# Bilinear features from 33 correlations of the value map instead of a second mixing convolution

## The chip, the cores and the metric

The kernel runs on one core of one Trainium2 chip, in float32 throughout. The metric is the device time of one execution in microseconds (us). Before the change three executions took 12944.30, 12963.82 and 12975.63 us, median 12963.82 us.

## The reference, cut to what matters

An input of 16 images of 56 x 56 tokens with 128 channels goes through four residual layers: windowed attention (stage 0), a triangle multiplication (stage 1), a Fourier attention block (stage 2) and a bilinear block (stage 3). The change touches stage 3, and how stage 1 gets four of its weights. Stage 3 for one image:

```python
xp = jax.nn.silu(x @ W1) @ W2                     # 128 q, 16 k, 16 v channels
q, k, v = l2norm(q per 16), l2norm(k), l2norm(v)  # 8 heads of q; k and v: 16 channels each
K_H1 = conv2d(k, H1_w, groups=16) + P1            # 3x7 window, 256 channels: (16, 16) per token
kernel = einsum('xnk,xkd->xnd', q, K_H1)          # (8, 16) per token
feature = conv2d(v, H2_w)                         # (v=16, d=16) per token
V_G = conv2d(v, G_w) + I                          # (v=16, w=16) per token
feature = einsum('xvw,xvd->xwd', V_G, feature)
out = einsum('xnd,xvd->xvn', kernel, feature)     # (16, 8) per token
```

Both convolutions of v are shared by all 16 value channels: every channel v is convolved with the same 16 filters H2 and the same 16 filters G. The feature is thus feature[w,d] = sum over v of (I[v,w] + sum_s G[w,s] v_v(x+s)) * (sum_t H2[d,t] v_v(x+t)). The part without I needs only sums over the channels, sum_v v_v(x+s) v_v(x+t): these are values at position x+s of a correlation map with the lag t-s. A 3 x 7 window has 5 x 13 lags, 33 of them up to sign.

## The kernel before, in words

Two images are worked on at a time, one in each of two **lanes** (lane 0: images 0, 2, ...; lane 1: images 1, 3, ...). A lane has its own large SBUF buffer (`arena`, 128 x 17152 float32, one buffer, given anew to every stage of every image), its own small buffers (`w2`, five of 128 x 512), its own PSUM banks (two of `psb`, one double bank `psd`) and its own DRAM tiles. The program is written image by image; a scheduler with a timeline model then sets the order of the instructions on each engine, and so interleaves the two lanes. Each engine, and each engine's DMA queue, takes its instructions in that order. DMAs that SyncE (SP) and ScalarE (ACT) ask for draw in turn on eight semaphores, DMAHW0 to DMAHW7, and one that gets a semaphore waits until the DMA that had it before, eight issues back, has landed. GpSimd's (POOL's) table DMAs have eight of their own.

Stage 3 cuts an image into seven chunks of 448 tokens (eight image rows). The steps by name, with line numbers of the kernel before:

- `project(q)` (1345 to 1401): normalizes, W1, SiLU, W2. The q channels go through `kept` (1338): a copy to SBUF by ACT and one DMA that writes them eight times to DRAM (`dy`, 1792 KB). The k and v channels are squared, summed, raised to the power -0.5 on POOL (417), scaled (1380), turned by TensorE (1388), and written by three ACT DMAs (1397), one per window row, into a zero-edged image in DRAM, `padded`.
- `spread(i, q)` (1403): four SP DMAs bring 84 shifted rows each of the k (i=0) or v (i=1) image into `im`, the moving operand of the convolutions.
- `conv(w, i, slot)` (1411): TensorE applies `l3wk` (k with H1 and P1), `l3wf` (v with H2) or `l3wg` (v with G and I) to 896 results per token, and ACT empties them into `zs` (1427). `l3wk` and `l3wg` run as groups of four 32-column matmuls side by side (`e.together`, lines 369 and 372); `l3wf` runs with all 128 columns (1420).
- `contract(y, z)` (1430): the per-token product and sum. Four SP DMAs (1439, 448 KB each) bring `dy` back as `rep`, replicated over partitions; four VectorE (DVE) multiplies of 128 x 1792 (1442) multiply it by `z`; sixteen 32-column matmuls with the constant `red` (369, 372) add up.
- `last(q, y, z)` (1457): the third contraction, transposes, scaling by the norm, residual and store.

Per chunk there are three contractions, chained: queries with zk, that with zf (the kernel with the feature's H2 factor), that with zg. Two of the results go through `kept` besides the queries, so each chunk has three `dy` writes and twelve `rep` reads. The loop of 1484 to 1500 spaces these over five rounds: chunk q is projected two rounds ahead, and contracted in rounds q, q+2 and q+4.

Stage 1 reads its weights `w1a`, `w1b`, `pout`, `gout` from the one weight tile `wgt` that is loaded at the start and stays in SBUF.

Of the kernel before, what the change touches and what calls it, by code (L numbers as in the profile page):

```python
# [36 lines left out]
F32 = mybir.dt.float32  # L37
# [55 lines left out]

def _constants():
# [31 lines left out]
    c["heads"] = np.kron(np.eye(8), np.ones((16, 1)))  # L126

# [78 lines left out]
def _weights(i):  # L206
# [15 lines left out]
    for n, (a, b) in zip("ab", cut):  # L222
        w["w1" + n] = np.concatenate([pw[:, a], pw[:, b], gw[:, a], gw[:, b]], 1)
    w["pout"] = g["L1_conv_p_out_w"].T
    w["gout"] = g["L1_conv_g_out_w"].T
# [48 lines left out]
    w["l3w2a"] = g["L3_conv_W2"][:128]  # L274
    w["l3w2b"] = np.pad(g["L3_conv_W2"][128:], ((0, 96), (0, 0)))
# [5 lines left out]
    wk3, wg3 = (np.zeros((P, 4, 2, 4, 8), np.float32) for _ in range(2))  # L281
    wf3 = np.zeros((P, 4, 16, 8), np.float32)
    for u in range(16):
        rows = slice(u % 4 * 21, u % 4 * 21 + 21)
        wk3[rows, u // 4, :, u % 4] = h1[u].reshape(2, 8, 21).transpose(2, 0, 1)
        wg3[rows, u // 4, :, u % 4] = gg.reshape(2, 8, 21).transpose(2, 0, 1)
        wf3[rows, u // 4, :, u % 8] = h2.reshape(16, 21).T
    wk3[84] = g["L3_conv_P1"][0].reshape(4, 4, 2, 8).transpose(0, 2, 1, 3)
    wg3[84] = g["L3_conv_I"][0].reshape(4, 4, 2, 8).transpose(0, 2, 1, 3)
    for n, v in (("l3wk", wk3), ("l3wf", wf3), ("l3wg", wg3)):  # L290
        w[n] = v.reshape(P, -1)
    return w, early, late
# [333 lines left out]
def _triangle(env):  # L626
# [5 lines left out]
    def layer_norm(chunk, dst, sqs, lw, lb):  # L632


        for q in range(NCH):
# [5 lines left out]
            nc.vector.tensor_copy(d, p[:, :CH])  # L641

# [22 lines left out]
    def run(b, xt):  # L665
# [3 lines left out]
        nc.gpsimd.memset(xh[:, NTOK:], 0.0)  # L669

# [6 lines left out]
        layer_norm(normed, xh, sqs, 0, 1)  # L677
# [5 lines left out]
        for part in range(2):  # L683
            for g in range(T // 8):
                p = e.psd()
                for i in range(8):
                    c0 = (8 * g + i) * T
                    for half, w in ((0, "w1a"), (64, "w1b")):
# [3 lines left out]
                            rhs=W(w).rearrange("p (k c) -> p k c", c=64)[:, :, HC * part : HC * part + HC],  # L692
# [34 lines left out]
        for q in range(NCH):  # L727
            s = slice(q * CH, (q + 1) * CH)
            pg, py = e.psb(), e.psb()
            mm(pg[:, :CH], lhsT=W("gout"), rhs=xh[:, s], start=True, stop=True)  # L730
            mm(py[:, :CH], lhsT=W("pout"), rhs=on[:, s], start=True, stop=True)
# [572 lines left out]
def _bilinear(env):  # L1304
# [6 lines left out]
    SPAN = 8 * PITCH  # L1311

# [3 lines left out]
    nc.gpsimd.memset(zeros[:, :part], 0.0)  # L1316
    for t in padded:
        for k in range(3):
            nc.sync.dma_start(out=t[:, k * part : (k + 1) * part], in_=zeros[:, :part])

# [4 lines left out]
    def run(b, xt):  # L1325
        nm, rs = e.group_norm(xt)
        ar = e.arena()
        kv_dram = padded[e.lane[0]]

        im = [ar[:, 4 * SPAN * k : 4 * SPAN * (k + 1)] for k in range(2)]  # L1330
        nc.gpsimd.memset(ar[64:P, 0 : 8 * SPAN], 1.0)
        zs = [ar[:, 3968 + k * 896 : 4864 + k * 896] for k in range(4)]
        reps = [ar[:, 7552 + k * 896 : 8448 + k * 896] for k in range(4)]
        prods = [ar[:, 11136 + k * 1792 : 12928 + k * 1792] for k in range(3)]
        norms = ar[:TT, 16512:16792]
        count = [0, 0, 0]

        def kept(p):
# [188 lines left out]
```

## Time and profile before

| | us |
|---|---|
| median of three runs | 12963.82 |
| the profiled execution | 12942.02 |
| its span, first to last instruction | 12940.2 |
| TensorE (PE) matmuls busy | 9941.9 (77%) |
| VectorE (DVE) busy | 9365.3 (72%) |
| ScalarE (ACT) busy | 3739.1 (29%) |
| GpSimd (POOL) busy | 2346.8 (18%) |
| DMA queue of SP | 823.91 MB, 19.1% of 16 DMA engines |
| DMA queue of ACT | 639.44 MB, 13.3% |
| DMA queue of POOL | 616.76 MB, 17.7% |
| DVE multiplies of the contractions (line 1442) | 2648.4, 1344 of 2019 ns |

The first column of the profile's page is busy time: an engine is busy while one of its instructions runs, and a PE that is busy need not be at its peak. The page also cuts the span into 40 slices and gives each engine's busy share in tenths; a view of windows gives the same in microseconds for stretches that one chooses. Every five slices (about 1612 us) one pair of images goes by: stages 0 and 1 (no DMA), stage 2 (the table DMAs of POOL), stage 3 (the DMAs of SP and ACT). Stage 3 of both lanes of a pair runs at the same time, from about 2650 to 3280 us for the second pair.

### The profile page before, as it was taken

How to read it: one execution, taken by the hardware profiler on the slowest of the kernel's cores; microseconds unless marked ns; L12 is line 12 of the kernel's file. 1: busy time of each engine (PE TensorE's matmuls, PEld its weight loads, DVE VectorE, ACT ScalarE, POOL GpSimd, SP SyncE). 2: the span in 40 equal slices, each digit the busy share in tenths (PEclk: the TensorE clock that was granted, in tenths of full speed). 3: DMA queues.
4: the chain of work that ended last, by engine and by line, in shares of the span. 5: the costliest groups of instructions: out<-in, count | busy, mean ns of one | idle time of the engine just before them, and what ended most of it. 6: DMA issues, size and time to landing. Idle time of an engine off the chain costs nothing. (4 is left out here: it accounts for less than half of the span.)

```text
span 12940.2 us, 198571 instructions
## 1 busy us (share of the span) xinstructions
PE 9941.9 (77%) x81312; PEld 5481.7 (42%) x81312; DVE 9365.3 (72%) x12257; ACT 3739.1 (29%) x6439; POOL 2346.8 (18%) x3131
## 2 busy tenths in 40 slices
PE   7787678876888767887788876878768887687876
PEld 4443254442544325443254432544325453254532
DVE  7775777757777577775877757777577775867757
ACT  4322142231422314223142231422314223142321
POOL 0133001330012300123101230012300123001230
PEclk9887888888988889888898888988889888898888
DMA  1255902659026590355903569035690356903469
GB/s 36 58 182 195 341 29 69 171 199 334 32 83 157 198 339 28 87 153 203 342 21 82 158 210 338 18 92 148 212 333 21 96 145 234 324 8 106 134 236 317
DMA packets 1090458, 2092.81 MB, mean 162 GB/s; under 512 B 97936, under 2 KB 973712, under 8 KB 1089296
## 3 DMA queue, kind: packets, MB, share of 16 engines
q1 hardware_dynamic: 560000, 823.91, 19.1%
q0 software_dynamic: 163840, 616.76, 17.7%
q10 hardware_dynamic: 365712, 639.44, 13.3%
q8 instruction: 644, 10.55, 0.3%
q14 instruction: 262, 2.15, 0.1%
HBM read 1412.69 MB, written 667.03 MB: 161 GB/s over the span
## 5 line engine op out<-in xcount | busy, mean ns | idle before, releaser
L1442 DVE TENSOR_TENSOR arena<-arena 128x1792 f32<-128x1792 f32 x1344 | 2648.4, 2019 | 652.5 <-PE psb L372 349.3
L1211 DVE TENSOR_TENSOR arena<-arena 112x1344 f32<-112x1344 f32 x1024 | 1563.3, 1552 | 322.4 <-DMA arena<-table 310.4
L372 PE MATMUL psb<-arena,cst 128*32 128x448 f32 x9792 | 1505.2, 649 | 0.0
L1209 POOL DMA_DIRECT2D arena<-table x2048 | 1050.7, 515 | 2206.3 <-DMA arena<-table 496.5
L369 PE MATMUL psb<-arena,cst 128*32 128x448 f32 x1408 | 792.3, 650 | 813.7 <-DVE arena L1442 760.4
L372 PE MATMUL psb<-arena 128*64 128x448 f32 (+2 forms) x4864 | 1248.5, 534 | 0.0
L369 PE MATMUL psb<-arena 112*64 112x448 f32 (+1 forms) x1280 | 689.0, 624 | 374.2 <-DVE arena L1104 201.9
L417 POOL TENSOR_TENSOR arena<-arena,power 112x32 f32<-112x32 f32 x224 | 828.6, 3718 | 119.8 <-DVE arena L1373 118.4
L372 PE MATMUL psd<-arena 112*64 112x224 f32 (+1 forms) x3072 | 725.6, 457 | 0.0
L372 PEld LDWEIGHTS psb<-arena 112*64 112x64 f32 (+1 forms) x4864 | 455.3, 155 | 526.8 <-issue 521.1
L1427 ACT COPY arena<-psd 128x896 f32<-128x896 f32 x336 | 304.1, 906 | 1236.1 <-DVE arena L1442 656.6
L369 PE MATMUL psd<-arena 112*64 112x448 f32 x1024 | 539.9, 612 | 133.3 <-DVE arena L1211 117.6
L369 PEld LDWEIGHTS psb<-arena,cst 128*32 128x32 f32 x1408 | 120.3, 118 | 1211.5 <-DVE arena L1442 966.4
L1104 DVE TENSOR_TENSOR arena<-w,coef 128x1792 f32<-128x1792 f32 x256 | 508.0, 2018 | 81.4 <-PE psb L372 71.0
L372 PEld LDWEIGHTS psb<-arena,cst 128*32 128x32 f32 x9792 | 360.6, 123 | 448.2 <-issue 427.4
L372 PE MATMUL psd<-arena,wgt 128*32 128x448 f32 x2688 | 502.8, 608 | 38.8 <-DMA arena<-padded 38.3
L689 PE MATMUL psd<-wgt,arena 128*64 128x128 f32 x7168 | 493.3, 283 | 49.3 <-DVE arena L701 38.9
L369 PE MATMUL psd<-arena,wgt 128*32 128x448 f32 x896 | 440.7, 611 | 79.9 <-DMA arena<-padded 42.2
L689 PEld LDWEIGHTS psd<-wgt,arena 128*64 128x64 f32 x7168 | 425.4, 139 | 179.5 <-issue 126.8
L918 PE MATMUL psb<-cst,arena 128*128 128x64 f32 (+1 forms) x2688 | 447.6, 340 | 54.3 <-ACT arena L928 25.6
L918 PEld LDWEIGHTS psb<-cst,arena 128*128 128x128 f32 x2688 | 439.0, 255 | 93.2 <-issue 50.6
L1341 ACT COPY w<-psb 128x448 f32<-128x448 f32 x336 | 178.7, 532 | 1006.5 <-PE psb L372 749.9
(305 smaller groups left out, 18845.8 us busy)
## 6 DMA issues: line engine op xcount, KB each, us to landing
arena<-table POOLq DMA_DIRECT2D x2048, 294.0 KB, 9.1
dy<-w ACTq DMA_DIRECT2D x336, 1792.0 KB
arena<-dy SPq DMA_DIRECT2D x1344, 448.0 KB
arena<-padded SPq DMA_DIRECT2D x896, 162.8 KB
w<-x SPq DMA_DIRECT2D x112, 224.0 KB
out<-w SPq DMA_DIRECT2D x112, 224.0 KB
padded<-w ACTq DMA_DIRECT2D x336, 62.0 KB
padded<-arena SPq DMA_DIRECT2D x6, 449.5 KB
```

The lines of the kernel that those rows point to most:

```text
L369: done = mm(**first)
L372: mm(**kw)
L417: ptt(dst, src, w, ALU.pow)
L689: mm(p[half : half + 64, i // 4, i % 4 * P : (i % 4 + 1) * P], lhsT=xh[:, c0 : c0 + 64], rhs=W(w).rearrange("p (k c) -> p k c", c=64)[:, : ...
L918: mm(p[:, 2 * i * nl : 2 * (i + 1) * nl], lhsT=src[:, t * P : (t + 1) * P], rhs=fc, start=True, stop=True)
L1104: tt(t4, bc(ys[c][:, l0 : l0 + 4, :], 1, 8), bc(coef[:, c, h0 : h0 + 8, l0 : l0 + 4], 3, T), ALU.mult,)
L1209: nc.gpsimd.dma_start(out=t[hh * T : (hh + 1) * T, :], in_=bc(tflat[q, two, hh], 0, T))
L1211: tt(t4, bc(x3[:, :, s], 1, 2), t4, ALU.mult)
L1341: nc.scalar.copy(t[:, :CH], p[:, :CH])
L1427: nc.scalar.copy(z, p[:, :, :CH])
L1442: tt(t4, bc(rep, 2, 2), bc(z, 1, 2), ALU.mult)
```

## The change

The contraction with zg goes. What it made is computed from the value map before any token's product is taken:

- W2's value columns are doubled: one copy keeps the plain v, one is multiplied by I at the start (`l3vt`, `l3i`), so that the H2 convolution works on v times I, and gives the I part of the feature by itself. `project` now carries 48 instead of 32 channels per token group, and writes the plain v by one more ACT DMA into a new DRAM tile, `values`, in eight copies, each shifted by one element against the one before.
- `correlate(q)`: one SP DMA brings the values of a chunk (128 partitions: 8 copies of 16 channels), six more bring 32 of the 33 lags, eight lags to a tile, straight from the shifted copies. ACT squares, DVE multiplies twice (128 x 992), and five matmuls with the constant `lag` add up the channels: 33 correlation rows of 496 elements, which ACT copies and writes to DRAM (`corr`).
- `gather(q)`: eight SP DMAs bring 126, 105 and 81 shifted rows of the correlations into three tiles `near`.
- `feature()`: the four `l3wf` matmuls as before, and six more with `quad` (products of G and H2, made by DVE at the start), added in the same PSUM banks; ACT empties them once.
- The loop does two contractions per chunk: queries with zk in round q, that with the feature in round q+3. `kept` is called twice per chunk instead of three times. `spread(0, q)` moves to the round's start, `gather` and `spread(1, .)` stand a round ahead of the `feature()` that reads them.
- Stage 1's four weights leave `wgt`. They are loaded for each image by one ACT DMA (128 x 768) into the stage's arena, asked for after the last chunk of the first layer norm.

The diff, cut to its core:

```diff
+        own = {n: whole[:, e.at["early"][n][1] - first :][:, : e.at["early"][n][2]] for n in ("w1a", "w1b", "pout", "gout")}
...
+        def load():
+            nc.scalar.dma_start(out=whole, in_=e.ins["early"][:, first : first + 768])
+
+        layer_norm(normed, xh, sqs, 0, 1, load)
...
-        nc.gpsimd.memset(ar[64:P, 0 : 8 * SPAN], 1.0)
+        nc.gpsimd.memset(ar[64:P, 0 : 11 * SPAN], 1.0)
+        near = [ar[:, (8 + k) * SPAN : (9 + k) * SPAN] for k in range(3)]
...
+            nc.scalar.dma_start(
+                out=planes(v_dram, (1 + 8 * q) * PITCH, ((VPLANE, D), (D * VPLANE - 1, 8), (1, SPAN))),
+                in_=bc(t[32:48], 1, 8),
+            )
...
+        def correlate(q):
+
+            at = (1 + 8 * q) * PITCH
+            one, sq = e.w2()[:, :SPAN], e.w2()[:, :SPAN]
+            nc.sync.dma_start(out=one, in_=planes(v_dram, at, ((0, 8), (VPLANE, D), (1, SPAN))))
+            act(sq, one, AF.Square)
+            acc = e.psb()
+            mm(acc[:33, :SPAN], lhsT=C("lag")[:, 132:165], rhs=sq, start=True, stop=False)
+            for two in (0, 2):
+                t = reps[count[1] % 4].rearrange("p (g t) -> p g t", g=2)
+                count[1] += 1
+                for g in range(2):
+                    k = 8 * (two + g)
+                    for j, n in ((0, 8),) if k < 16 else ((0, 5), (5, 3)):
+                        dr, dc = RUNS[k + j]
+                        nc.sync.dma_start(
+                            out=t[D * j : D * (j + n), g],
+                            in_=planes(v_dram, at + dr * PITCH + dc, ((VPLANE, D * n), (1, SPAN))),
+                        )
+                tt(t, t, bc(one, 1, 2), ALU.mult)
+                for g in range(2):
+                    o = 33 * (two + g)
+                    mm(acc[:33, :SPAN], lhsT=C("lag")[:, o : o + 33], rhs=t[:, g], start=False, stop=two + g == 3)
+            y = e.w2()
+            nc.scalar.copy(y[:33, :SPAN], acc[:33, :SPAN])
+            nc.scalar.dma_start(out=planes(r_dram, at, ((RPLANE, 33), (1, SPAN))), in_=y[:33, :SPAN])
+
+        def gather(q):
+
+            for n, parts in enumerate(GATHER):
+                row = 0
+                for s0, first, last, c0, m in parts:
+                    nc.sync.dma_start(
+                        out=near[n][row : row + (last - first) * m],
+                        in_=planes(r_dram, first * RPLANE + (8 * q + s0) * PITCH + c0, ((RPLANE, last - first), (1, m), (1, SPAN))),
+                    )
+                    row += (last - first) * m
...
+        def feature():
+
+            p, rows, wt = e.psd(), shifted(1), W("l3wf")
+            for h in range(2):
+                for g in (2 * h, 2 * h + 1):
+                    mm(p[:, h, :CH], lhsT=wt[:, g * P : (g + 1) * P], rhs=rows[g], start=g == 2 * h, stop=False)
+            for n in range(3):
+                for h in range(2):
+                    mm(p[:, h, :CH], lhsT=quad[:, n, h], rhs=window_of(near[n]), start=False, stop=n == 2)
+            return emptied(p, 1)
...
-        queries, kern, feat = {q: project(q) for q in range(2)}, {}, {}
-        spread(0, 0)
-        for q in range(NCH + 4):
-            if 0 <= q - 4:
-                last(q - 4, *feat.pop(q - 4))
+        queries, kern = {q: project(q) for q in range(2)}, {}
+        for q in range(NCH + 3):
+            if 0 <= q - 3:
+                last(q - 3, kern.pop(q - 3), feature())
+            if q < NCH:
+                spread(0, q)
             if q + 2 < NCH:
                 queries[q + 2] = project(q + 2)
+            if q < NCH:
+                correlate(q)
             if 0 <= q - 2 < NCH:
-                zf, zg = conv("l3wf", 1, 0), conv("l3wg", 1, 1 + q % 2)
-                if q - 1 < NCH:
-                    spread(1, q - 1)
-                feat[q - 2] = kept(contract(kern.pop(q - 2), zf)), zg
+                gather(q - 2)
+                spread(1, q - 2)
             if q < NCH:
-                zk = conv("l3wk", 0, 3)
-                if q + 1 < NCH:
-                    spread(0, q + 1)
-                kern[q] = kept(contract(queries.pop(q), zk))
-            if q == 0:
-                spread(1, 0)
+                kern[q] = kept(contract(queries.pop(q), conv()))
```

`PITCH` is 62 (56 tokens and 6 of padding), `SPAN` is 8 rows of it, 496 elements; `RUNS` lists the lags in the order of the shifted copies and `GATHER` the rows that each `near` tile takes.

## The prediction

> **What bounds the kernel now.** I read the slices of the page first: PE, DVE and DMA over the span.
>
> ```profile
> span 12940.2 us, 198571 instructions
> ...
> PE   7787678876888767887788876878768887687876
> ...
> DVE  7775777757777577775877757777577775867757
> ...
> DMA  1255902659026590355903569035690356903469
> ```
>
> Every five slices a pair of images goes by, 1612 us. No engine is near 100% throughout, but DMA is at 9 in one slice of five and at 0 in another. The windows of the third pair, 160 us each, tell the stages apart (columns: PE, PEld, DVE, ACT and POOL busy, granted clock, DMA share, GB/s):
>
> ```profile
> 3520.00:3680.00 160.00, 144.03 (x1658) 105.51 (x1658) 90.29 (x158) 70.08 (x99) 3.17 (x7) 0.87 0.04 9
> 3680.00:3840.00 160.00, 121.63 (x642) 59.79 (x642) 127.59 (x145) 34.13 (x58) 26.64 (x53) 0.85 0.32 87
> 3840.00:4000.00 160.00, 132.74 (x888) 69.57 (x890) 133.42 (x118) 28.25 (x53) 55.82 (x110) 0.91 0.71 200
> 4000.00:4160.00 160.00, 134.84 (x957) 73.29 (x956) 126.51 (x166) 30.24 (x57) 54.74 (x102) 0.84 0.74 190
> 4160.00:4320.00 160.00, 119.00 (x1037) 80.90 (x1038) 101.21 (x226) 74.45 (x132) 24.67 (x22) 0.82 0.12 41
> 4320.00:4480.00 160.00, 113.11 (x692) 55.24 (x694) 92.57 (x133) 44.92 (x80) 64.02 (x30) 0.81 0.75 258
> 4480.00:4640.00 160.00, 120.36 (x780) 50.85 (x772) 98.68 (x72) 30.41 (x51) 34.17 (x15) 0.86 0.97 340
> 4640.00:4800.00 160.00, 111.50 (x788) 39.09 (x788) 140.07 (x86) 24.01 (x36) 8.01 (x4) 0.87 0.98 350
> ```
>
> Stages 0 and 1 (first row, and 132.05 in the window before) keep PE busy 0.86 of the time; stage 2 (three rows) 0.81, with DVE as high; the seam (fifth row) 0.74; stage 3 (the last three) only 0.72, and there the 16 DMA engines stand at 0.97 and 0.98, moving 340 to 350 GB/s. So stage 3 is bound by DMA, the rest by PE and DVE together. The chain of waits agrees: between 12500 and 12700 us half of it is DMA (`dy<-w` 24%, `arena<-padded` 15%, `padded<-w` 6%, `arena<-dy` 5%). Its longest pieces there:
>
> ```profile
> 12580.46 12.59 DMA padded<-w
> 12594.27 20.11 DMA dy<-w
> ...
> 12615.76 8.04 DMA arena<-padded
> 12623.87 14.44 DMA dy<-w
> ...
> 12642.23 5.05 DMA arena<-padded
> ```
>
> **DMA, part by part.** Queue 1 (SP) took 19.1% of 12940 = 2472 us for 823.91 MB, 3.0 us per MB; queue 10 (ACT) 1721 us for 639.44 MB, 2.7. Per chunk one `dy` write of 1792 KB (1.835 MB) and four reads of 448 KB (1.835 MB) go: 205.5 MB each over 112 chunks, 553 + 617 = 1170 us. Added per chunk: values 0.254 MB and lags 1.016 MB (128 and 4 x 128 rows of 1984 B), gathered rows 312 x 1984 B = 0.619 MB, all on SP: 211.6 MB, 635 us; shifted copies 0.254 and correlations 0.065 MB on ACT: 35.8 MB, 96 us; the triangle weights 6.3 MB, 17 us, in stage 1, where DMA is idle. Net 1170 - 748 = 422 us over all 16 engines, 53 us per pair out of some 520.
>
> **DVE.** The rows for it and for PE, each shape by itself:
>
> ```profile
> L1442 DVE TENSOR_TENSOR arena<-arena 128x1792 f32<-128x1792 f32 x1344 | 2648.4, 2019 | 652.5 <-PE psb L372 349.3 <-DMA arena<-dy 215.8 <-ACT arena L1427 71.0
> ...
> L372 PE MATMUL psb<-arena,cst 128*32 128x448 f32 x9792 | 1505.2, 649 | 0.0
> ...
> L372 PE MATMUL psd<-arena,wgt 128*32 128x448 f32 x2688 | 502.8, 608 | 38.8 <-DMA arena<-padded 38.3
> ...
> L1420 PE MATMUL psd<-arena,wgt 128*128 128x448 f32 x896 | 383.0, 571 | 35.5 <-ACT arena L1427 21.6 <-DMA arena<-padded 9.8 <-DMA arena<-dy 3.3
> ```
>
> Four of twelve multiplies per chunk go, 8.08 us. Two of 992 elements come, between 1084 ns (the 896-element row of line 883) and 2019 ns: 1.2 us each. Splitting line 1380 in two adds 0.25 us. Net -5.4 us per chunk, -605 us: DVE falls from 9365 to about 8760.
>
> **PE.** A matmul shows as two instructions. A contraction's matmuls run four abreast: 1505.2 us, 96% of it contractions (the rest layer norms), over 336 gives 4.3 us each; a `wg` convolution 502.8 / 224 = 2.24. So 6.5 us go per chunk. What comes has all 128 rows and no neighbour abreast: `quad` 12 instructions at line 1420's 383.0 / 896 = 0.43 us, 5.1 us; `correlate` 10 at 0.43 x 496 / 448, 4.7 us. Net +3.3 us per chunk, **+372 us**: PE goes from 9942 to about 10,314. Below, at eight of line 1420 in 3.27 us (its best group) it is +240; above, at the mean durations 571 and 649 ns, +840. So the change takes work from DMA and DVE and gives some to PE, which was already the busiest.
>
> **ACT, POOL, SP.** ACT loses a `kept` copy (532 ns) and a 906 ns copy per chunk and gets a square and a copy of about 0.55 us each: nothing, hidden by an ACT 29% busy. POOL's larger memset adds about a microsecond per image, before stage 3's first DMA. SP issues 31 DMAs per stage-3 chunk where it issued 22: eight gathers at line 1406's 0.76 us and seven value loads at about 0.4 are 9 us, less four at 0.37: +7.5 us per chunk, 52 us per image on a queue that has some 500. It costs nothing unless SP stands in a wait; see the rivals. The start gets about 5 MB of zeros and a few small DVE steps: 10 to 20 us, once, beside image 1's lane.
>
> **What moves: the lanes.** The built program's order, engine by engine, can be read without a chip. Before, both lanes stand in the same stage: DVE's instructions on image 10's stage 3 alternate with image 11's stage 3. In the changed program they drift apart within four pairs, and then image 11's stage 3 stands beside image 12's stages 0 and 1, image 12's stage 2 beside image 13's 0 and 1, image 12's stage 3 beside image 13's stage 2. Two stages 3 no longer meet, so DMA is no longer asked for 520 us of work in one 600 us stretch: it is 233 us beside stages 0 and 1, which have none, and 233 + 143 (the table's 17.7% / 16 images) beside stage 2. The price is at the end: image 15's stage 3 is alone.
>
> **The sum**, against the profiled execution's 12942 us (span 12940). With DMA unloaded, PE's work over PE's attainable share sets the time. Stage 3 of one image is about 245 us of PE (35 us per chunk). Alone, at stage 3's share of 0.72, it lasts 340 us. The other 10,314 - 245 = 10,069 us run at a mix: per pair two windows at 0.86 as now and the other eight, seams and stage 3 among them, at stage 2's 0.81, mean 0.82 (now 0.77). 10,069 / 0.82 + 340 = **12,620**. The median of the runs shown is 22 us above the profiled execution, which is less than I can resolve; I keep **12,620 us**, 2.6% below the median.
>
> **Two rules.** The built program swaps ACT's function tables more often when the lanes stand in different stages: 214 loads against 119. A load has a row of its own:
>
> ```profile
> L655 ACT ACT_TABLE_LOAD x32 | 41.1, 1283 | 0.6
> ```
>
> By it 95 more loads are 122 us of ACT over the whole span, hidden. The Trainium skill, "ScalarE: Activation LUTs", section "What ACT_TABLE_LOAD costs", adds a drain of about 1380 ns to each switch; by that it would be an estimated 250 us on ACT, still under its idle time. Against the change speaks "DMA: Bandwidth & Descriptors", section "Anatomy of one DMA": every DMA pays about 2 us however small it is. By that rule 1373 more DMAs are an estimated 2.7 ms in a row, or 340 us if eight are always in flight, and the sum would be near 12,960. Here the DMAs of stage 3 take far longer than that to land (5 to 20 us in the chain above), because they queue for bandwidth.
>
> **Rivals.**
>
> *Faster than forecast.* Lanes in different stages fill each other's gaps so well that PE reaches the 0.86 of stages 0 and 1 throughout: 10,069 / 0.86 + 340 = **12,050**. For it: the windows at 0.97 DMA have PE and DVE both idle a fourth of the time. Against: the seam, where stages 2 and 3 do stand beside each other, has 0.74.
>
> *Slower: landings in a row.* In the built order SP's gathers wait for the correlations of the same round to be written, and the loads of the next contraction stand behind them in SP's queue. Each round then has lag loads landing, multiplies (2.4 us), matmuls (4.7), a copy, the write landing, and 23 issues (about 14 us). With landings of 5 us, a round is some 32 us, 320 us for ten rounds: hidden beside a stage of about 500. With 12 us as in the chain above it is 46, and with waits for semaphores (every DMA waits for the one eight issues back, a big `dy` write included) 55: 550 us per image, over the 500 of its neighbour. It decides from about 50 us a round. Then the seam's share holds: 10,069 / 0.78 + 340 = **13,250**, and at today's 0.77 13,420.
>
> *Nothing.* DMA relief and PE's addition cancel: 12,940. It needs a share of 0.80 exactly.
>
> **How the numbers follow.** Chances: forecast (12,300 to 12,900) 0.44, the faster rival 0.24, the slower 0.27, nothing 0.05. Runs of this kernel tell 0.2%, 26 us, from no change. Faster 0.68, same 0.05, slower 0.27. The range leaves out the last tenths on both sides: below, 0.86 without PE's upper cost, 12,000; above, a share of 0.78 as the slower rival has it, 13,250. The forecast's own side, faster, is 12,000 to 12,900.
>
> **What would show it.** Right: the DMA row no longer at 9 beside 0; windows with stage 3 in one lane and stage 1 or 2 in the other at PE 0.80 or more; line 1442's successor at 896 multiplies; PE busy near 10,300. The slower rival: SP's waits on its gathers for the correlation write, and PE idle before the `quad` matmuls for `corr`. Wrong altogether: PE above 10,800, so that the unpacked matmuls are what was mis-sized, or a granted clock below 0.85 with them.

## The result, and the profile after

The changed kernel took 14154.08 us (median of four executions, 14114.22 to 14192.28) beside 12954.06 us for the kernel before on the same chip: a ratio of **1.0929** [1.0889, 1.097]. The forecast, 12,620 us, has the wrong sign, and 14,154 lies above the range. The profiled execution has a span of 14112.3 us. In what follows 1% of the kernel before is called a point, about 129 us; differences between kernels are taken between their ratios.

The page of the changed kernel, first its slices (PE, DVE and DMA busy in tenths, forty slices):

```profile
span 14112.3 us, 194846 instructions
...
PE   6887788777787777877777777777778777777765
...
DVE  6784567746676556755567565765657656576553
...
DMA  1247704566045660366512745327364174541745
```

DMA has no slice at 9 after the change. In the first half it still goes by pairs, in the second the pattern dissolves: the lanes have drifted apart, as the built order said. That much of the forecast came true. But lower digits are not less work for the DMA engines. The two queues that the change touches, SP's (q1) and ACT's (q10), with their packets, their MB and the share of 16 engines' span that the packets took:

```profile
q1 hardware_dynamic: 563776, 834.93, 19.5%
...
q10 hardware_dynamic: 272592, 475.48, 10.8%
```

Their bytes fell about as forecast, from 1463 to 1310 MB. The time of the 16 engines did not: 30.3% of 14,112 us is 4276, where 32.4% of 12,940 was 4193. The forecast had 422 us less. SP's queue went from 3.0 to 3.3 us per MB, ACT's from 2.7 to 3.2.

And PE did not rise: 10770.9 us of 14112 is 0.763, before it was 0.768. And the loss is there from the start: the first pair, whose lanes still stand in the same stages, has 711 us from the first to the last DVE instruction of stage 3, against 614 before.

The groups of the page that answer to the ones shown of before (busy and mean of one, then idle time ahead of them and what ended most of it):

```profile
L1578 DVE TENSOR_TENSOR arena<-arena 128x1792 f32<-128x1792 f32 x896 | 1796.4, 2021 | 1360.6 <-DMA arena<-dy 739.5
...
L1517 PE MATMUL psb<-arena,cst 128*33 128x496 f32 x896 | 495.8, 689 | 206.6 <-DVE arena L1514 206.4
...
L1514 DVE TENSOR_TENSOR arena<-arena,w 128x992 f32<-128x992 f32 x224 | 263.5, 1189 | 535.0 <-DMA arena<-values 392.7
L1563 PE MATMUL psd<-arena,quad 128*128 128x448 f32 x1344 | 564.6, 559 | 25.3 <-DMA arena<-corr 21.8
```

The counts and durations are near the forecast: 896 multiplies, lag multiplies of 1189 ns (1.2 us forecast), `quad` 564.6 / 112 = 5.0 us per chunk (5.1). What was not forecast stands behind the second bar. A third fewer multiplies have twice the idle time ahead of them, 1361 us where it was 652, and the `dy` reads that DVE waits for cost 740 us where they cost 216, although DMA has no full slice any more.

Two PE groups, each shape by itself:

```profile
L410 PE MATMUL psb<-arena,cst 128*32 128x448 f32 x6656 | 985.5, 630 | 0.0
...
L1502 PE MATMUL psb<-w,cst 128*33 128x496 f32 x224 | 175.2, 878 | 166.1 <-ACT w L1500 157.9 <-DVE w L1601 8.2
```

The contraction's matmuls went down (9792 instructions to 6656, by 520 us). The last line is the matmul of the square. It stands apart from the other eight of `correlate`, waits for ACT, and takes longer than they do, 878 ns on average where theirs take 689: (495.8 + 175.2) / 112 = 6.0 us per chunk for `correlate`, where 4.7 were forecast.

The windows of a stretch in which one lane is in stage 3 and the other passes through stages 0 and 1, and of the end, where image 15 is alone (columns as before: PE, PEld, DVE, ACT, POOL, clock, DMA share, GB/s):

```profile
11880.00:12040.00 160.00, 113.56 (x833) 61.04 (x834) 80.92 (x155) 53.76 (x95) 42.37 (x29) 0.82 0.41 124
12040.00:12200.00 160.00, 123.45 (x768) 58.63 (x766) 88.71 (x115) 44.66 (x69) 16.68 (x10) 0.87 0.57 177
12200.00:12360.00 160.00, 134.02 (x1082) 73.46 (x1084) 80.77 (x72) 30.35 (x45) 7.53 (x3) 0.86 0.61 192
13760.00:13920.00 160.00, 96.55 (x370) 35.34 (x374) 46.07 (x39) 16.58 (x28) 17.78 (x10) 0.73 0.58 176
13920.00:14080.00 160.00, 97.47 (x422) 34.21 (x412) 69.56 (x46) 15.62 (x25) 7.53 (x3) 0.78 0.64 199
```

Mixed, PE has 0.71, 0.77 and 0.84 of 160 us, where 0.80 or more was the sign of being right; alone 0.60 and 0.61, where 0.72 was forecast. DMA is at 0.4 to 0.6 and nobody is busy all the time: nothing is saturated. The timeline of one round of stage 3 in that stretch shows what the engines do instead (start, duration, engine, line, and in brackets the idle time before):

```profile
12063.69 0.61 SPq L1499 DMA_DIRECT2D w<-values  x1
...
12070.52 0.62 ACT L1500 ACTIVATE w<-w 128x496 f32<-128x496 f32 x1 [2.32 <-DMA w<-values]
...
12076.44 0.32 ACTq L1476 DMA_DIRECT2D values<-w  x1
...
12080.87 2.69 SPq L1510 DMA_DIRECT2D arena<-values  x6
...
12086.35 1.19 DVE L1514 TENSOR_TENSOR arena<-arena,w 128x992 f32<-128x992 f32 x1 [0.26 <-DMA arena<-values]
...
12091.29 3.52 PE L1517 MATMUL psb<-arena,cst 128*33 128x496 f32 x8
...
12093.17 5.99 SPq L1575 DMA_DIRECT2D arena<-dy  x3
...
12094.84 0.56 ACT L1519 COPY w<-psb 33x496 f32<-33x496 f32 x1 [8.95 <-PE psb L1517]
...
12096.75 2.02 DVE L1578 TENSOR_TENSOR arena<-arena 128x1792 f32<-128x1792 f32 x1 [7.03 <-DMA arena<-dy]
```

SP asks for the six lag loads 4.4 us after ACT asked for the write of `values`, as soon as that has landed. Until then SP has stood still for 16.6 us, since it issued the value load at 12063.69. Its waits for that write are the largest of those that the change brought (in total, times, longest):

```profile
SPq L1510 <- DMA values<-w: 1199.4, 74, 30.6
```

The lag loads land 3 to 4 us later, DVE multiplies, PE sums up, and only then, at 12093.17, do `dy` reads go out for the contraction, because the lag products hold two of the four buffers that `dy` reads use, and stand before them in SP's queue (SP's waits for line 1517 are 604 us in all). DVE's next contraction multiply has waited 7.03 us.

### The profile page after: what moved, and what is told of

Read it like the earlier page. It is cut to its first block, busy times and chain, and to the rows that moved or that the text cites. A ratio compares the mean times of both kernels' runs of the same rounds, so it can differ in the third digit from the quotient of the medians.

```text
span 14112.3 us, 194846 instructions
## 1 busy us (share of the span) xinstructions
PE 10770.9 (76%) x78404; PEld 5772.4 (41%) x78404; DVE 8796.0 (62%) x12156; ACT 3839.2 (27%) x6534; POOL 2338.7 (17%) x3131
## 5 line engine op out<-in xcount | busy, mean ns | idle before, releaser
L1578 DVE TENSOR_TENSOR arena<-arena 128x1792 f32<-128x1792 f32 x896 | 1796.4, 2021 | 1360.6 <-DMA arena<-dy 739.5
L410 PE MATMUL psb<-arena 112*64 112x224 f32 (+2 forms) x4864 | 1264.2, 533 | 0.0
L410 PE MATMUL psb<-arena,cst 128*32 128x448 f32 x6656 | 985.5, 630 | 0.0
L407 PE MATMUL psb<-arena,cst 128*32 128x448 f32 x960 | 539.0, 649 | 302.0 <-DVE arena L1578 253.0
L1517 PE MATMUL psb<-arena,cst 128*33 128x496 f32 x896 | 495.8, 689 | 206.6 <-DVE arena L1514 206.4
L1514 DVE TENSOR_TENSOR arena<-arena,w 128x992 f32<-128x992 f32 x224 | 263.5, 1189 | 535.0 <-DMA arena<-values 392.7
L735 PE MATMUL psd<-arena 128*64 128x128 f32 x7168 | 525.0, 295 | 91.2 <-DVE arena L747 84.7
L1563 PE MATMUL psd<-arena,quad 128*128 128x448 f32 x1344 | 564.6, 559 | 25.3 <-DMA arena<-corr 21.8
L735 PEld LDWEIGHTS psd<-arena 128*64 128x64 f32 x7168 | 450.7, 148 | 205.8 <-issue 119.2
L638 PE MATMUL psb<-cst,arena 128*49 128x128 f32 x2048 | 355.7, 328 | 194.3 <-DVE arena L633 136.1
L410 PEld LDWEIGHTS psd<-arena 112*64 112x64 f32 x3072 | 299.1, 156 | 300.8 <-issue 294.7
```

Source lines behind the costliest of these rows:

```text
L407: done = mm(**first)
L410: mm(**kw)
L638: nc.tensor.transpose(p[:WIN, i * P : (i + 1) * P], s3[:, 4 * g + i, :], C("ident"))
L735: mm(p[half : half + 64, i // 4, i % 4 * P : (i % 4 + 1) * P], lhsT=xh[:, c0 : c0 + 64], rhs=own[w].rearrange("p (k c) -> p k c", c=64)[:, ...
L1517: mm(acc[:33, :SPAN], lhsT=C("lag")[:, o : o + 33], rhs=t[:, g], start=False, stop=two + g == 3)
L1563: mm(p[:, h, :CH], lhsT=quad[:, n, h], rhs=window_of(near[n]), start=False, stop=n == 2)
```

## The experiments

Three theories at the start: **C**, the waits inside a round (a value write, then lag loads, then the correlation write, then gathers); **P**, the added PE work at the unchanged share; **D**, the drift of the lanes.

**Order within a round.** Gather and `spread(1)` go first, then `correlate`, then `project`, so that each waits for what was written a round earlier:

```diff
-            if q + 2 < NCH:
-                queries[q + 2] = project(q + 2)
-            if q < NCH:
-                correlate(q)
             if 0 <= q - 2 < NCH:
                 gather(q - 2)
                 spread(1, q - 2)
+            if q < NCH:
+                correlate(q)
+            if q + 2 < NCH:
+                queries[q + 2] = project(q + 2)
```

> The changed kernel with the steps of a round in another order: gather and the value spread first, then correlate, then project, so that each reads only what the round before wrote; same work. Theory C (a round of one lane is a chain: project, value write, lag loads, correlation matmuls, correlation write, gather, 50 to 75 us a round) expects the round to shrink to 40 to 50 us and the time to fall by 500 to 1100 us, to 13050 to 13650. Theory P (TensorE has 829 us more busy time and runs at an unchanged share of 0.76) expects no change, 14000 to 14300. Theory D (the lanes stand in different stages, which costs) expects no change as long as the lanes still drift apart.

14057.17 us, 1.0846 [1.082, 1.0872]: 0.8 of 9.3 points. The gathers' wait for the correlations is not the main cause. (The lag loads' wait for the write of the values is not gone by this order: in the same order with the lanes in step, below, SP still stands 456 us for it, where it stands 510 in the kernel's own order.)

**Narrow matmuls.** The PE work added goes almost entirely:

```diff
-mm(acc[:33, :SPAN], ..., rhs=t[:, g], ...)
+mm(acc[:33, :62], ..., rhs=t[:, g, :62], ...)
-mm(p[:, h, :CH], lhsT=quad[:, n, h], rhs=window_of(near[n]), ...)
+mm(p[:, h, :T], lhsT=quad[:, n, h], rhs=window_of(near[n])[:, :1], ...)
```

> The changed kernel with the quad matmuls over 56 of 448 columns and four of five correlation matmuls over 62 of 496: leaves out 7/8 of these sums, keeps every DMA, wait and order of the loop. TensorE loses some 840 us of busy time (7.5 us per chunk). Theory P: 840 / 0.76 = 1100 us less, about 13050. Theory C: the 7.5 us lie in the chain of a round, some 50 us per image in a lane of eight images: 400 us less, about 13750. Theory D: under 200 us less.

13924.27 us, 1.0746 [1.0725, 1.0767]. PE is busy for 10296.0 us, 475 less, and 1.8 points, 237 us, went with it: half a microsecond for each, and PE's share fell to 0.74. PE's work alone does not set the time.

**The triangle weights alone.** The kernel before, with the per-image load on ACT's queue:

```diff
-                            rhs=W(w).rearrange("p (k c) -> p k c", c=64)[...],
+                            rhs=own[w].rearrange("p (k c) -> p k c", c=64)[...],
+        def load():
+            nc.scalar.dma_start(out=whole, in_=e.ins["early"][:, first : first + 768])
+        layer_norm(normed, xh, sqs, 0, 1, load)
```

> The kernel before with the one part alone that stage 1's weights are loaded for each image by ACT. All theories: the same as before within 0.5%, 12900 to 13020; if ACT stands in the DMA's wait for its semaphore, up to 100 us more.

12930.01 us, 0.9982 [0.9963, 1.0001]: nothing, as forecast.

**Without correlations.** The changed kernel without `correlate` and `gather`; the `quad` matmuls read constants:

```diff
-            if q < NCH:
-                correlate(q)
             if 0 <= q - 2 < NCH:
-                gather(q - 2)
                 spread(1, q - 2)
```

> The changed kernel without correlate and gather: leaves out the correlations, the near tiles hold constants; the value write and the quad matmuls stay. Takes away 15 SP DMAs, an ACT DMA, five matmuls (4.4 us) and two multiplies per chunk. Theory C: the chain of a round is gone, 12700 or less. Theory P: 496 us of matmuls less at 0.76, about 13500. Theory D: 13500 to 14000.

13164.07 us, 1.0158 [1.0138, 1.0179]. The two cost 7.7 points. But the kernel is still 1.6% slower than before, with a third of the contractions gone and little added: `quad`, the plain values with their write, and the triangle loads. Its lanes drift too.

**The lanes held in step.** Both kernels get a wait between pairs: an image's load takes its bias (here zero-times-last-value added) from a tile that the last chunk of an image of the pair before has written:

```diff
+    turn = [persistent(f"turn{k}", [P, 1]) for k in range(2)]   # both copied from bout0
-            act(xt[...], p[:, :CH], AF.Identity, bias=W("bout0"))
+            act(xt[...], p[:, :CH], AF.Identity, bias=turn[(b // 2 + 1) % 2])
+            if q == NCH - 1:                                     # in last()
+                own = e.turn[b // 2 % 2]
+                nc.vector.scalar_tensor_tensor(own, y[:, 0:1], 0.0, own, ALU.mult, ALU.add)
```

> The kernel before with one dependency added: a pair's loads wait for the last contraction of both images of the pair before, so that no pair starts ahead. It loses the overlap of a pair's end with the next one's start, some 50 to 80 us at each of seven seams. All theories: 13300 to 13550. It is the measure for the next run.

> The changed kernel with the same dependency added: the lanes can't drift apart by more than a pair. Theory D (drift costs): the ratio to the kernel before with the same dependency is 0.97 to 1.03, about 13000 to 13700. Theories C and P, and any that puts the loss in stage 3 itself: the ratio stays at 1.08 to 1.10, 14400 to 14800.

> The reordered rounds of the first experiment with the same dependency. If drift hid what the reordering gains (theory C behind theory D), 300 us or more below the changed kernel in step; if a round's chain doesn't matter, within 150 us of it.

Before in step: 13091.37 us, 1.0125 [1.0092, 1.0157]; the wait itself costs 1.25 points in a kernel whose lanes are in step anyway. After in step: 13887.99 us, 1.0745 [1.0714, 1.0776], 1.8 points *less* than without the wait. Reordered in step: 13866.00 us, 1.0721 [1.0677, 1.0765], no different. So drift costs at least 1.8 points, and 3 if the wait costs in this kernel what it costs before. The other 6 points need no drift. They lie in one place: from the first to the last DVE instruction of a stage, in the median of eight pairs, before and after in step have 418 and 427 us for stages 0 and 1, 715 and 718 for stage 2, and **614 and 708 for stage 3** (at the seams two stages overlap). Two windows of the second pair's stage 3, before in step:

```profile
2860.00:3000.00 140.00, 111.24 (x734) 49.93 (x735) 88.42 (x69) 31.21 (x53) 42.15 (x20) 0.88 0.94 332
3000.00:3140.00 140.00, 99.95 (x674) 37.92 (x674) 104.30 (x66) 22.51 (x35) 15.54 (x7) 0.85 1.00 359
```

and after in step:

```profile
2980.00:3120.00 140.00, 105.96 (x493) 45.59 (x491) 54.13 (x58) 25.66 (x47) 44.27 (x21) 0.84 0.85 268
3120.00:3260.00 140.00, 105.47 (x469) 36.73 (x465) 62.16 (x48) 19.16 (x32) 16.20 (x8) 0.88 0.84 268
```

DMA's share falls (0.85 and 0.84, where it was 0.94 and 1.00), but not its work: over the whole execution the packets of SP and ACT take 30.1% of 13,909.9 us, 4187, and before in step 32.0% of 13,143.4, 4206. About the same engine time is spread over a longer stage. PE stands as it stood, DVE falls from 0.63 and 0.75 to 0.39 and 0.44. All further runs are in step, so that only stage 3 differs.

**What in stage 3.** Theory **S**: `dy` reads come late because the new loads share SP's queue and their buffers. Four kernels: the narrow matmuls again; without correlations; the new loads on another queue; the lag products in a buffer of the contraction's products, so that the multiply, not the matmul, frees the shared buffer.

```diff
-                        nc.sync.dma_start(            # value load, lag loads, gathers
+                        nc.gpsimd.dma_start(
```

```diff
-                tt(t, t, bc(one, 1, 2), ALU.mult)
+                made = prods[count[2] % 3][:, : 2 * SPAN].rearrange("p (g t) -> p g t", g=2)
+                count[2] += 1
+                tt(made, t, bc(one, 1, 2), ALU.mult)
```

> The quad matmuls get 56 columns instead of 448 and four of the five correlation matmuls 62 instead of 496, in the changed kernel with its lanes held in step (13,888 us). Left out: most columns of the bilinear features. It takes about 36 us of PE per image out of stage 3, 72 us of the 95 to 110 us by which a pair's stage 3 is longer than before's in step. Theory P (PE's added matmuls lie on the path of stage 3): 8 x 72 = 580 us go, 13,310. Theory S (the dy reads stand behind the new loads in SP's queue and come just in time, so DVE waits for them): under 150 us go, 13,740 or more, and DVE's wait for dy reads in a stage 3 stays near 124 us.

> The changed kernel in step without correlate and gather; the quad matmuls stay and read zeros. Left out: correlations and gathered rows. Theory S: SP's queue is free of the new loads, stage 3 falls back to about 610 us a pair or below, 13,090 to 13,200 in all. Theory P: only the 4.4 us of correlation matmuls per chunk leave the path, 112 x 4.4 = 490 us, 13,400. If stage 3 falls under before's, DMA relief is worth something once the new loads are gone, and the time is under 13,050.

> The value load, the lag loads and the gathers of the changed kernel in step are issued by POOL instead of SP; nothing else changes. Theory S: dy reads are again asked for as soon as a buffer is free; DVE's wait for them in one stage 3 falls from 124 us to under 50, and the time to 13,300 to 13,500. Theory P: unchanged, 13,840 to 13,900. A third: POOL's own work (memset and power of project) now stands behind waiting loads, and the time rises above 14,000.

> The lag products go into a buffer of the contraction's products instead of staying in the buffer that the dy reads share, so that DVE's multiply frees it and not the correlation matmul 5 to 10 us later. In step. Theory S in the form that the held buffers delay the dy reads (SP's waits for PE line 1517, 50 us in one stage 3): 50 us a pair at most, 13,500 to 13,800. Theory P, or S by order alone: 13,840 to 13,930.

Narrow: 13754.80 us, 1.0626 [1.0582, 1.067], 1.2 points for 515 us of PE; P is out here too. Without correlations: **12628.26 us, 0.975** [0.9715, 0.9784]: 10 points less than after in step, 3.8 less than before in step, stage 3 at 561 us in the median. Loads on POOL's queue: 14086.28 us, 1.0883 [1.0852, 1.0914], slower, as the third theory had it; POOL then stands 1013 us at the gathers, waiting for correlations to be written, with `project`'s power step behind it. Products apart: 13880.92 us, 1.0719 [1.0686, 1.0751], nothing. So the cost is `correlate` and `gather`, and S in the two forms tried fails. With the new steps away the kernel beats the one before, and only there DMA is really relieved: the packets of SP and ACT take 27.4% of 12,624.6 us, 3459.

DVE's waits (in total, times, longest) in after in step:

```profile
DVE arena L1582 <- DMA arena<-dy: 807.6, 282, 8.9
DVE arena L1582 <- PE psb L410: 552.0, 182, 9.7
...
DVE arena L1518 <- DMA arena<-values: 360.0, 117, 13.4
```

and in the kernel without correlations:

```profile
DVE arena L1583 <- PE psb L410: 637.9, 224, 11.4
...
DVE arena L1583 <- DMA arena<-dy: 28.6, 22, 6.3
```

The wait for `dy` falls from 808 to 29 us. Before in step has

```profile
DVE arena L1446 <- DMA arena<-dy: 198.6, 103, 9.7
```

**Which half.** Only `correlate`; only `gather`; all of both with fewer DMAs of almost the same bytes; and the narrow kernel with the lag multiplies cut as well.

```diff
-                    for j, n in ((0, 8),) if k < 16 else ((0, 5), (5, 3)):
+                    for j, n in ((0, 8),):                           # 4 lag loads
-                for s0, first, last, c0, m in parts:
+                for s0, first, last, c0, m in (((0, 15, 33, 0, 7),), ((1, 18, 33, 0, 7),), ((0, 3, 15, 0, 7),))[n]:
```

```diff
-                tt(t, t, bc(one, 1, 2), ALU.mult)
+                tt(t[:, :, :62], t[:, :, :62], bc(one[:, :62], 1, 2), ALU.mult)
```

> The changed kernel in step without gather (8 DMAs per chunk); correlations are computed and written, the quad matmuls read zeros. Left out: the gathered rows. With both parts it takes 13,888 us, with neither 12,628: 1260 us to be shared out. Theory W (the work of correlate on PE, DVE and ACT and the waits between them): correlate has nearly all, 13,600 to 13,850. Theory N (each of the 16 DMAs per chunk costs the same, 0.70 us): half goes, 13,260. Theory G (the gather's wait for the written correlations): most goes, under 13,000.

> The other half: the changed kernel in step with gather but without correlate, so that the gathered rows are zeros from the start. Left out: the correlations. Theory W: 12,650 to 12,800. Theory N: 12,628 + 112 x 8 x 0.70 = 13,260. Theory G: 12,650 to 12,800 too, since no wait for a write is left.

> The changed kernel in step with 4 lag loads instead of 6 and 3 gathers instead of 8 per chunk, of at least the same bytes; all matmuls and multiplies stay. Changed: the rows of the shortened loads are those of other lags. Theory N: 112 x 7 x 0.70 = 550 us less, 13,340. Theory W: 13,820 to 13,900.

> The narrow kernel in step (13,755 us) with the lag multiplies cut from 992 to 124 elements as well. Left out: most columns of the bilinear features. DMAs and waits are all there, the added work of PE and DVE is nearly gone. Theory W: 1 us per multiply and the waits for it go, 13,400 or less. Theories N and G: within 100 us of 13,755.

`correlate` alone 13751.69 us, 1.0602 [1.0539, 1.0666]; `gather` alone 12835.89 us, 0.991 [0.9881, 0.994]; fewer DMAs 13723.54 us, 1.0587 [1.0539, 1.0635]; small work 13716.34 us, 1.0585 [1.0526, 1.0645]. `gather` costs 1.4 to 1.6 points, `correlate` 8.4 to 8.5. The number of DMAs is worth 1.6 points, the work on PE and DVE 1.6, the `quad` matmuls' share in it included. Most of `correlate` is neither. Theory G is out, and N and W each have a small part.

**Which part of correlate.** The loads read a copy in DRAM that nobody writes in the loop; the square and the first matmul move behind the multiplies, so that a PSUM bank and ACT are held for less; and the six lag loads with their buffers go, the multiplies squaring the value tile.

```diff
-in_=planes(v_dram, at, ...), in_=planes(v_dram, at + dr * PITCH + dc, ...)
+in_=planes(still, at, ...), in_=planes(still, at + dr * PITCH + dc, ...)
```

```diff
+            act(sq, one, AF.Square)                                  # after both multiplies
+            acc = e.psb()
+            for k, t in enumerate(ts + [sq]):
+                mm(acc[:33, :SPAN], lhsT=C("lag")[:, 33 * k : 33 * k + 33], rhs=t, start=k == 0, stop=k == 4)
```

```diff
-                        nc.sync.dma_start(out=t[D * j : D * (j + n), g], ...)
-                tt(made, t, bc(one, 1, 2), ALU.mult)
+                tt(made, bc(one, 1, 2), bc(one, 1, 2), ALU.mult)
```

> The changed kernel in step whose value load and lag loads read a third copy in DRAM that is written once, with zeros, before the first image, so that they wait for no write of the same round; all DMAs, multiplies and matmuls stay. Left out: the true values. Theory T (the trip of the values through DRAM inside a round: write, landing, loads, and SP, ACT, DVE and PE standing in turn at the loads): most of correlate's 1050 us goes, 12,900 to 13,200. Theory L (the loads themselves, in whatever place, and the engines that wait for their landing): 13,700 to 13,890.

> The changed kernel in step, its computation whole: in correlate the square and the first matmul move behind the lag multiplies, so that ACT does not stand at the square while the value load is on its way (ACT's wait for it is 93 us in one stage 3) and one of the lane's two PSUM banks is held only for the five matmuls and the copy. Theory B (the bank and ACT are held over the loads): 13,300 to 13,600. Theory T: 13,840 to 13,930.

> The changed kernel in step with correlate's six lag loads and their two shared buffers left out: the multiplies square the value tile into buffers of the contraction's products, as in the run with the products apart (13,881 us). Left out: 32 of the 33 correlations. Value load, multiplies, matmuls and the write of the correlations stay. Theory L (the lag loads: SP's time, the two of four buffers that the dy reads lose, DVE standing at their landing): DVE's wait for dy reads falls under 50 us a stage 3, and the time to 13,000 to 13,250. Theory T (the chain of the values through DRAM, which stays with the value load): 13,600 or more. Between them both have a share.

Still values: 13562.66 us, 1.0478 [1.0444, 1.0511], 2.7 points, between the ranges of T and L; DVE's wait for `dy` is still 894 us there, and in the run with the products apart it was 418 without any gain, so that wait goes with the loss but does not measure it. Late sums: 14114.58 us, 1.0878 [1.0842, 1.0915], 1.3 points slower; so holding a bank and ACT over the loads is not shown to cost anything. No lag loads: 13385.41 us, 1.034 [1.0289, 1.0391], 3.8 points less than the same kernel with them, and 4.3 more than with `gather` alone, again between the two ranges. DVE's waits there:

```profile
DVE arena L1574 <- PE psb L410: 606.8, 186, 14.6
DVE arena L1574 <- PE psb L1513: 346.0, 93, 10.4
DVE arena L1510 <- DMA w<-values: 289.9, 71, 9.3
...
DVE arena L1574 <- DMA arena<-dy: 86.8, 36, 8.4
```

With the lag loads gone the wait for `dy` is 87 us, and the one for the lag loads is gone; what is left of `correlate` shows as waits for its matmuls (346) and for the value load (290). The first of these comes in part from the experiment itself, which puts the lag products among the contraction's products: with the products apart and the lag loads still there it is 245 us, in after in step it does not show. No version of the changed kernel whose computation is whole beats the one before; the fastest, products apart and the reordered one in step, stand at 1.072.

## Why the prediction was wrong

In points of before, by the runs in step, from 1.0125: minus 3.8 for what the change removes; plus 1.6 for `gather`; plus 4.3 for `correlate` without its lag loads; plus 3.8 for these; 0.3, within the error, between the kernel with the products apart and the change in step; plus 1.8 when the lanes are let go. That is 1.0929. Each difference carries some 0.5 to 0.7 points, and those within `correlate` overlap, since its loads, its waits and its work stand in one chain. Each kernel was also ordered anew by the scheduler: in the narrow one in step SP's DMAs stand in another order than in after in step from the 93rd on, though its edit touches none of them. So each difference holds the edit and the order that came with it, and a small one can't be put down to the edit alone.

- **DVE and the durations.** Right: DVE lost 569 us where 605 were forecast, and the new multiplies and `quad` took what was said.
- **"Net 1170 - 748 = 422 us over all 16 engines."** Wrong in time, right in bytes: the packets of SP and ACT took 83 us more than before, in step 19 us less. I had priced every byte at its queue's average. In the trace of the change, ACT's packets of 1984 bytes took 318 us, where those of before, all from `padded`, took 66; so the shifted copies and the correlations cost about 250 us, 7 us per MB, where 96 were forecast. The `dy` write that went away costs 2.7 to 2.9 us per MB, and the SP packets that stayed became dearer: those of 1792 bytes went from 2.9 to 3.3 us per MB. Why is not shown.
- **"With DMA unloaded, PE's work over PE's attainable share sets the time."** This step failed, in its condition and in its rule. DMA was not unloaded, as just said. And I raised the share from 0.77 to 0.82, where without the tail it came to (10,771 - 267) / (14,112 - 480) = 0.77. The share is no stock that a kernel attains once DMA stands back. Before and after in step have about the same DMA time and differ by 6.2 points; the fewer DMAs and the still values take 1.6 and 2.7 points off at 30.5% of 13,703.5 us, 4180, and 30.7% of 13,574.3, 4167, again the same DMA time. What changed is who waits for whom: the change added a chain of waits, the values' trip through DRAM with the lag loads behind it, that the sum had at nothing. PE's work moved the time by half its size or less: two runs that took 475 and 515 us of PE away gave 237 and 154 us. In the forecast's own sum the miss of 1492 us is 820 for the share, 530 for PE's work and 140 for the tail.
- **PE's +372.** Measured +829, just under the upper bound given, 840. (The lower bound of 240 is a slip: the best group's 0.41 us per matmul gives 320.) The new matmuls are 564.6 + 495.8 + 175.2 = 1236 us, where 9.8 us per chunk, 1098, were forecast: `quad` is as forecast, but `correlate`'s matmuls take 0.55 us each, and the square's 0.78, where 0.47 was forecast for all. Less went than forecast, too: 520 us of contractions and 161 of convolutions (502.8 to 341.3), 681 instead of 728. The rest is stages 0 to 2, whose matmuls are the same: per image 76.5, 94.8 and 242.5 us of PE became 85.2, 98.5 and 251.6. In step they are 76.0, 92.8 and 249.2, so most of it comes with the drift. (By stage the parts add up to more than the whole, since a moment in which two stages run side by side counts for both.) I had added up work as if its duration did not depend on what the other lane does.
- **"SP costs nothing unless it stands in a wait."** It stands in one, for a write of `values` that was asked for in the same round: 16.6 us in the round shown, the last 4.4 of them for the landing, and 1199 us in all, 510 in step. With that wait taken away 2.7 points went. (That SP issues 31 DMAs per chunk where it issued 22 does not fit together: 15 come and 4 go, as the price beside it has it.) By its row numbers, chunk q's lag loads need nothing of chunk q+2's write, for which they wait in the timeline; that the two footprints overlap as ranges of addresses would explain it, but this is argued, not shown.
- **Drift.** Right that it comes, wrong that it is a gain. Two lanes in stage 3 fill each other's waits: 708 us for two images in step. One lane alone took about 480 us for one, as the tail shows. Why the mixture with stages 0 to 2 does not make up for it I have not shown.
- **The slower rival** had the mechanism, landings in a row, and its condition was met: in the stretch from 11,983 to 12,318 us the first lag multiplies of seven rounds are 50, 52, 76, 72, 40 and 45 us apart. Its place was wrong. It named the gathers' wait for the correlations; that is small, 0.8 points by the order alone, and PE stood only 21.8 us before `quad` for `corr`. Its time, 13,250, was 900 us short as well. The lag loads and the trip of the values ahead of them decide. And it took landings of 12 us as the danger, where they were short: with the DMA engines at 0.4 to 0.6, `dy` reads landed in 3.8 us in the median (11,800 to 12,360 us) after 7.4 before (4320 to 4800 us), `dy` writes in 8.0 after 13.1, and lag loads in 3.5. A chain of short landings was enough. In the round shown SP and DVE stand in it, with the `dy` reads and the next multiply behind them.
- **Triangle weights, ACT's tables.** The weights cost nothing, as forecast. 214 table loads came as counted in the built order; with the lanes in step there are 100. So they are one of the things that drift's 1.8 points may hold, and no run takes them apart.
- **"Wrong altogether."** Both signs stand at their edge: PE has 10,771 us, where over 10,800 was the sign, and the granted clock is 0.848 to 0.854 in the four executions, where below 0.85 was. Both looked for a mis-sized matmul. The narrow kernels, with a lower clock still (0.827 in the first) and less PE work, are faster, so neither is the main part of the loss.

What stays open: how the cost of the lag loads divides between DVE's place in the queue, the shared buffers and SP's order. The two kernels that took away one of these each gained nothing, but the one that moved the loads brought a new wait on POOL. Buffers of their own for the lag loads were not tried. Nor is it shown why late sums lose. A rival was not tested: with the new steps the packets of SP and ACT take 4187 us in step, without them 3459, so of the 147 us by which a pair's stage 3 is longer (708 against 561), up to 91 could be the DMA engines' own time. It can't be the loss against the kernel before, whose packets take as long; how much of the 10 points it is would need a kernel that moves fewer bytes through the same chain.

The Trainium skill, "DMA: Bandwidth & Descriptors", section "Anatomy of one DMA", gives a fixed cost of about 2 us per DMA, as a fit to DMAs that GpSimd issues. The 784 DMAs that one run saved are SP's; if the figure held for them too, with eight in flight, that would be an estimated 196 us. The run gave 1.6 points, about 205 us. That is the same size and no proof of the rule, and it is a sixth of what `correlate` and `gather` cost.

## What to carry to other kernels

A busy share below one is not room that fills up when the busiest neighbour is relieved: before dividing work by a hoped-for share, follow one round through all engines and ask which queue a new DMA round trip stands in, and what stands behind it. Price DMA by the kind of transfer and not by the queue's mean per MB: 153 MB less were moved here in the same engine time. A change that saves bytes and multiplies but adds a write to DRAM, loads of what was written and another write in every round can lose though no engine and no queue is full. Two interleaved lanes in the same latency-bound stage can be better neighbours than two in different ones; hold them in step once to see what their order is worth.

## What the runs showed of the hardware

- Loads of 155 to 448 KB still take 3.5 to 3.8 us to land in the median where the DMA engines stand at 0.4 to 0.6; at 0.75 to 0.98, 448 KB took 7.4.
- With 56 and 62 columns instead of 448 and 496 in the new matmuls the granted clock of the whole execution was lower: 0.827, 0.837 and 0.834 in the three narrow kernels, 0.848 to 0.866 in the profiled executions of the kernels whose computation is whole. With the correlation matmuls left out altogether and the lanes in step it was 0.875.
- ACT's write of the eight shifted copies (248 KB) landed after 4.4 us in all seven rounds between 11,800 and 12,360 us. It and the write of the correlations took about 7 us of the 16 engines per MB, the `dy` write 2.9.
- POOL can ask for these loads, but its `project` steps then wait behind them: 1.4 points slower than with SP.
